# A mixing matrix from split factors: three products of rounded parts in place of one product in full precision

## The chip, the core and the metric

The kernel runs on one core of a Trainium2 chip. The metric is the device time of one execution in microseconds (us), taken as the median over several executions. A second number, the span, comes from one execution under the hardware profiler: it runs from the first to the last instruction of the program, and is a little shorter than the time of the same execution. Five engines work side by side, each through its own queue in order: the tensor engine (PE, with its weight loads shown apart as PEld), VectorE (DVE), ScalarE (ACT), GpSimd (POOL), and SyncE (SP), which here issues nearly all DMAs.

## The reference

The input x has four blocks (b) of 512 rows and 256 columns. Two layers follow each other, each of a mixer `s` and a gated feed-forward net `g`, joined as `x + s * silu(g)`.

```python
# layer 0, mixer: one step of a recurrence that starts from zero
xi = (x @ W_in.T).reshape(b, l, NC, D)[..., None]
nr, ni = B_real * xi, B_imag * xi          # the old state is zero
y = jnp.sum(C_real * nr - C_imag * ni, axis=-1)
out = y.reshape(b, l, NC * D) @ W_out.T
s = x + rmsnorm(out) * norm_w
# both layers, feed-forward net (fwht: a Walsh-Hadamard transform over the 1024 hidden columns)
hidden = fwht(silu(x @ W1.T) * (x @ W3.T))
g = hidden @ W2.T
```

Here x is already layer-normalized. Since the state begins at zero, the sum over the 16 state entries is a number for each of the 512 inner columns: `g[c] = sum(C_real * B_real - C_imag * B_imag)`. The mixer is therefore a single matrix of 256 by 256, `m = W_in.T @ diag(g) @ W_out.T`, which doesn't depend on x. The kernel computes m once, on the chip, and all four blocks use it. Layer 1 has an attention as its mixer.

## The kernel before, in words

**Split numbers.** Most products are made from pairs: a float32 array is rounded to a narrower matmul format (`F32R`), the high part, and the rest is stored as a low part of the same format. `split` (L59 to L62) does this with an ACT copy for the high part and a DVE subtraction for the low. `mm3` (L80) multiplies two pairs in three products: high by high, then high by low and low by high. In the profile all matmuls and transposes have the line L70 and all splits the lines L61 and L62, so that one goes by the names of tiles.

**Layer 0.** `ffn` treats one block in eight chunks of 128 hidden columns. For chunk c it makes two products (`f_0gu` and so on, the digit naming the block), puts a silu on one (L523), multiplies by the other (L524), splits the result into `hh` and `hl`, and feeds both to the down product `f_0dn`. Beside this, at two slots in each chunk, `Beside` runs steps of other tasks, in the given order, and spreads them by the counts that are passed with them.

In block 0 the first of these tasks is `prep_first`, which prepares weights. It is a generator made of two others:

- `prep_w2` applies the Hadamard transform to W2. For each half of its 256 columns it has three butterfly steps on DVE (`w2b`, L151 and L152), for the second half a split (`w2bh`, `w2bl`), and then two products by the Hadamard matrix (`w2ps`), each split into `w2h` and `w2l`.
- `prep_m` makes g on DVE (`cb` L203, `cbd` L205, `g` L207), scales the rows of W_out by it on ACT (`wg`, L210), and then calls `product_of_weights`: eight matmuls of plain float32 tiles (`mps<-wg,win`), and a split of the result into `mh` and `ml`.

After `prep_first` comes `mixer(0)`: it multiplies the block by m with `mm3` (`o`), copies the result to `osb` (ACT, L719), takes the squares of its rows on ACT (`junk`, L721), the power on POOL (`ssr`, L723 and L724), scales `osb` on DVE (L726) and adds it to `xn` (L729). Then `norm(0, 1)` normalizes block 1 (`ln_1st`, `xn`, L272 to L279), transposes it on PE (`xt_1tp`) and splits it into `xt`, the operand of all products of block 1. In block 0 four low halves of the hidden tiles (`early`, L540) are made late.

**Layer 1's weights.** While layer 0 runs, `prep_s` loads W1 and W3 of layer 1 in four quarters (`sraw`), adds and subtracts blocks (`ssum`), splits (`sp`) and writes the pairs to DRAM (`s<-sp`); `load_s` reads them back (`sw<-s`) into the buffers that the weights of layer 0 leave.

**What sets the order.** In layer 0 the program order is not the order of the queues. The kernel is built with a scheduler, which places the instructions on each engine by a model of times of its own; `after(...)` pins a few. A change in the program text can so rearrange queues far behind it. From the last down products of layer 0 on, PE's order is fixed by hand (`in_line`, L66 to L69). Buffers come from rings: tag `t4` has ten buffers of 4 KB for each partition (win, wout, wg, w2bh, sraw and many others), the PSUM tag `ms` three (`w2ps`, `mps`, `o`, the transposes), and `gu` three. A tile can be written only when the tile before it in its buffer has been read for the last time.

The order of the tasks around m, in `prep_first`, is:

```python
        for _ in range(2):
            next(steps)          # two of the butterfly steps of W2's second half
            yield
        product = prep_m(*raw_m)
        next(product)            # g and wg
        for _ in range(2):
            next(steps)          # third butterfly step; split into w2bh, w2bl
            yield
        load_x(1)
        next(product)            # mps, mh, ml
        yield
        yield from steps         # the two w2ps of the second half
```

Of the kernel before, what the change touches and what calls it, by code (L numbers as in the profile page):

```python
# [11 lines left out]
F32 = mybir.dt.float32  # L12
# [3 lines left out]
F32R = mybir.dt.float32r  # L16
AF = mybir.ActivationFunctionType
ALU = mybir.AluOpType
# [3 lines left out]
P = 128  # L22
D = 256
# [12 lines left out]
def kernel(ctx: ExitStack, tc: tile.TileContext, a: dict, out: bass.AP):  # L36
    nc = tc.nc

    wp = ctx.enter_context(tc.tile_pool(name="weights", bufs=1))
    act = ctx.enter_context(tc.tile_pool(name="act", bufs=2))  # L40
    dram = ctx.enter_context(tc.tile_pool(name="dram", bufs=2, space=bass.MemoryType.DRAM))
    ps = ctx.enter_context(tc.tile_pool(name="ps", bufs=2, space=PSUM))

    def t4(name, shape, dt=F32):
        return act.tile(shape, dt, tag="t4", name=name, bufs=10)
# [10 lines left out]
    def psum(name, shape, tag="ms", bufs=3):  # L56
        return ps.tile(shape, F32, tag=tag, name=name, bufs=bufs)

    def split(src, hi, lo, engine=nc.vector):  # L59

        h = nc.scalar.copy(hi, src)  # L61
        return h, engine.tensor_tensor(lo, src, hi.bitcast(F32), ALU.subtract)  # L62
# [5 lines left out]
    def in_line(call, *args, **kwargs):  # L68
        with tc.issue_after(line["last"].ins) if line["fixed"] and line["last"] else nullcontext():  # L69
            ins = call(*args, **kwargs)  # L70
        line["last"] = ins
        return ins

    def matmul(*args, **kwargs):
        return in_line(nc.tensor.matmul, *args, **kwargs)
# [4 lines left out]
    def mm3(o, terms):  # L80

        seq = [(l[0], r[0]) for l, r in terms]
        for l, r in terms:
            seq += [(l[0], r[1]), (l[1], r[0])]
        for n, (l, r) in enumerate(seq):
            ins = matmul(o, l, r, start=n == 0, stop=n == len(seq) - 1)
        return ins
# [4 lines left out]
    def x_slot(name, shape):  # L92
        return wp.tile(shape, F32, tag="x", name=name, bufs=B)

    def load_x(b, nt=NT, queues=(nc.sync,)):
        xs[b] = x_slot(f"x{b}", [P, NT, D])
        src = a["x"][b].rearrange("(t p) d -> p t d", p=P)
        for t in range(0, NT, nt):
            queue = queues[t // nt % len(queues)]
            queue.dma_start(xs[b][:, t : t + nt, :], src[:, t : t + nt, :])  # L100
# [38 lines left out]
    def prep_w2(layer, raws, dst, scratch):  # L139

        w2h, w2l = dst
        for half in range(2):
            ds_ = slice(half * P, (half + 1) * P)
            cur = raws[half]
            for st, h in enumerate((1, 2, 4)):
                nxt = scratch(f"w2b{st}_{layer}_{half}", [P, NH, P])
                cv = cur.rearrange("p (g two h) d -> p g two (h d)", two=2, h=h)
                nv = nxt.rearrange("p (g two h) d -> p g two (h d)", two=2, h=h)  # L150
                nc.vector.tensor_tensor(nv[:, :, 0], cv[:, :, 0], cv[:, :, 1], ALU.add)  # L151
                nc.vector.tensor_tensor(nv[:, :, 1], cv[:, :, 0], cv[:, :, 1], ALU.subtract)  # L152
                cur = nxt
                yield

            native = layer == 0 and half == 0
            if not native:
                bh = t4(f"w2bh_{layer}_{half}", [P, NH, P], F32R)
                bl = t4(f"w2bl_{layer}_{half}", [P, NH, P], F32R)
                split(cur, bh, bl)  # L160
                yield
            for q in range(2):
                o = psum(f"w2ps_{layer}_{half}_{q}", [P, NH // 2, P])
                qs = slice(q * NH // 2, (q + 1) * NH // 2)
                if native:
                    matmul(o, had_f, cur[:, qs, :], start=True, stop=True)
                else:
                    matmul(o, had, bh[:, qs, :], start=True, stop=False)
                    matmul(o, had, bl[:, qs, :], start=False, stop=True)
                split(o, w2h[:, qs, ds_], w2l[:, qs, ds_])  # L170
                yield
# [4 lines left out]
    def w2_tiles(layer):  # L176
        return w2_tile(f"w2h_{layer}"), w2_tile(f"w2l_{layer}")

    def product_of_weights(name, lhsT, rhs, nk):

        hi = wp.tile([P, 2, D], F32R, name=f"{name}h")
        lo = wp.tile([P, 2, D], F32R, name=f"{name}l")
        o = psum(f"{name}ps", [P, 2, D])
        for i in range(2):
            for k in range(nk):
                matmul(
                    o[:, i, :], lhsT(k, i), rhs(k), start=k == 0, stop=k == nk - 1
                )
        split(o, hi, lo)
        return hi, lo  # L190

    def load_m():
        win = t4("win", [P, 4, D])
        wout = t4("wout", [P, 4, D])
        nc.sync.dma_start(bc, a["bc"])
        nc.sync.dma_start(wout, a["w_outT"].rearrange("(c p) o -> p c o", p=P))
        nc.sync.dma_start(win, a["w_in"].rearrange("(c p) i -> p c i", p=P))
        return win, wout

    def prep_m(win, wout):  # L200

        cb = wp.tile([P, 4, 2, DS], F32, name="cb")
        nc.vector.tensor_tensor(cb, bc[:, :, 0:2, :], bc[:, :, 2:4, :], ALU.mult)  # L203
        cbd = wp.tile([P, 4, DS], F32, name="cbd")
        nc.vector.tensor_tensor(cbd, cb[:, :, 0, :], cb[:, :, 1, :], ALU.subtract)  # L205
        g = wp.tile([P, 4], F32, name="g")
        nc.vector.tensor_reduce(g, cbd, AX.X, ALU.add)  # L207
        wg = t4("wg", [P, 4, D])
        for c in range(4):
            nc.scalar.mul(wg[:, c, :], wout[:, c, :], g[:, c : c + 1])  # L210
        yield
        first["m"] = product_of_weights(
            "m", lambda k, i: win[:, k, i * P : (i + 1) * P], lambda k: wg[:, k, :], 4
        )
        yield

    def sl(i):
        return slice(i * P, (i + 1) * P)
# [240 lines left out]
    def after(ins):  # L459
        return tc.issue_after(ins.ins) if ins else nullcontext()  # L460
# [444 lines left out]
    def call(f, *args):  # L905
        f(*args)
        yield
# [26 lines left out]
    raw_m = load_m()  # L934
# [3 lines left out]
    first = {"table": None}  # L938
# [15 lines left out]
    def prep_first():  # L954
        steps = prep_w2(0, raw2, w2, x_slot)
        with after(first["w13"][1]):
            next(steps)
        yield
        for _ in range(4):
            next(steps)  # L960
            yield
        with after(first["silu"]):
            nc.scalar.copy(had, had_f)
        for _ in range(2):
            next(steps)
            yield
        product = prep_m(*raw_m)
        next(product)
        for _ in range(2):
            next(steps)  # L970
            yield
        load_x(1)
        next(product)
        yield
        yield from steps
# [15 lines left out]
    for b in range(B):  # L991
        tasks = []
        if b == 0:
            prep = prep_first()
            next(prep)
            tasks.append((prep, 11))
        if b:
            tasks.append((call(gate_all, f"g0_{b - 1}", dn, xns[0, b - 1], xs[b - 1]), 1))
        tasks.append((mixer(b), MIXER))
        if b + 1 < B:  # L1000
            if b:
                load_x(b + 1)
            if b == 2:
                tasks.append((prep_s(0), 4))
            tasks.append((norm(0, b + 1), NORM))
        if b == 0:
            early = w2_tile("early0"), w2_tile("early1")
            spare = [
                [early[i][:, 2 * c : 2 * c + 2, :].rearrange("p a d -> p (a d)") for i in range(2)]
                for c in range(NH // 2)  # L1010
            ]
        if b == 1:
            raw2_1 = load_w2(1)
            w2_1 = w2_tiles(1)
            tasks.append((prep_w2(1, raw2_1, w2_1, t4), W2P))
            tasks.append((prep_second(), 5))
        if b == 2:
            tasks += [(prep_s(1), 4), (norm(1, 0), NORM), (prep_s(2), 4)]
        if b == 3:
            atts = [Attention(0)]  # L1020
            at = atts[0]
            parts = run(at.xt_half, 0), run(at.xt_half, 1), at.xt, at.scaled, at.split_sums
            tasks += [(call(f), 1) for f in parts]
            norms = {1: norm(1, 1)}
            tasks.append((prep_s(3), 4))
        bg = Beside(*tasks)
        if b == 0:
            dn = ffn("f0_0", xTs[0, 0], w13, w2, bg.slot, NH, spare, parts=2, behind=True)
        else:
            tail = [run(atts[0].tq, j) for j in range(2)] if b + 1 == B else []  # L1030
            dn = ffn(f"f0_{b}", xTs[0, b], w13, w2, bg.slot, tail=tail)
        bg.finish()
# [33 lines left out]
    for b in range(B):  # L1066
# [15 lines left out]
        if not final:  # L1082
# [4 lines left out]
            c = Attention(b + 1)  # L1087
# [93 lines left out]
```

## Time and profile before

| what | value |
|---|---|
| time, median of 3 executions | 363.11 us (362.93 to 363.39) |
| the profiled execution: time | 362.72 us |
| the profiled execution: span | 360.9 us |
| DVE busy / ACT busy | 79% / 55% of the span |
| granted clock of PE | 1.00 throughout |
| eight products for m (`mps`), 16 records on PE | 26.4 to 31.4 us, beside other matmuls |
| `wg` on ACT, four of 128x256 | 24.65 to 26.36 us |
| split of m: `mh`, `ml` | 31.41 and 32.03 us |
| first product `o` with m | 36.34 us |
| first product of block 1 (`f_1gu`) | 51.49 us |
| loads of `sraw`, issued by SP | 82.41, 104.41, 132.84 and 158.48 us, landing 4.4 us later |

The page of a profile gives busy times by engine, and groups of instructions with their counts and mean lengths. The timeline lists instructions of one engine in order of time: start, length, engine, line, operation, the tile written and the tiles read, shape and count; in brackets the idle time of the engine before it and what ended it. The chain of waits follows the work that ended last back from the end: at each step to what released it, or to the instruction before it on its engine. An FP32 matmul shows as two records in this trace, a matmul of split numbers as one.

### The profile page before, as it was taken

Reading aid. Unit: us, or ns where it says so; the run is one execution under the profiler, and the core shown is the slowest. Engines: PE = TensorE matmul, PEld = TensorE weight load, DVE = VectorE, ACT = ScalarE, POOL = GpSimd, SP = SyncE. Lnnn points to the kernel's source line nnn. Section 1 sums busy time; section 2 is a strip of 40 time slices with the busy share of each in tenths; the row PEclk is TensorE's granted clock in tenths of the full one; section 3 lists DMA queues with packets and bytes.
Section 4 is the critical chain, followed back from the end, with each engine's and each line's share of the span. In section 5 each row is a group of like instructions: output and inputs, shape, how many; then the busy total and the mean of one; then the engine's idle time right before and its main releaser. Section 6 shows DMA issues by size and latency. Waiting matters only on the chain.

```text
span 360.9 us, 6262 instructions
## 1 busy us (share of the span) xinstructions
PE 354.3 (98%) x2469; PEld 327.9 (91%) x2469; DVE 286.1 (79%) x592; ACT 197.5 (55%) x372; POOL 19.0 (5%) x22
## 2 busy tenths in 40 slices
PE   8999999999999999999999999999999999999995
PEld 6878999888988898888999999999999999999995
DVE  6897868996679938898987957989679888568646
ACT  4665436274454335465467655576555676446443
POOL 1000201100011000100100001100011000000000
PEclk9999999999999999999999999999999999999999
DMA  7935000301063217637257135661554635345401
GB/s 228 346 108 186 3 0 2 116 0 60 0 196 155 118 52 236 237 130 254 85 206 261 49 157 205 223 226 79 203 205 152 215 162 203 136 149 193 194 2 58
DMA packets 16284, 52.25 MB, mean 145 GB/s; under 512 B 1632, under 2 KB 7936, under 8 KB 16256
## 3 DMA queue, kind: packets, MB, share of 16 engines
q1 hardware_dynamic: 15968, 51.60, 39.8%
q8 instruction: 19, 0.31, 0.3%
q10 hardware_dynamic: 288, 0.26, 0.2%
q14 instruction: 9, 0.07, 0.1%
HBM read 42.40 MB, written 9.45 MB: 144 GB/s over the span
## 4 chain that ended last, share of the span: by engine, by line
PE 78%; DVE 16%; ACT 2%; DMA 1%; issue 1%; POOL 1%; DVEq 0%; SPq 0%; ACTq 0%
PE f_0gu L70 6%; PE f_1gu L70 6%; PE f_0dn L70 5%; PE f_2dn L70 5%; PE f_3dn L70 5%; PE f_1dn L70 5%; PE f_3gu L70 5%; PE pv L70 4%; PE f_2gu L70 3%; PE tq L70 2%; PE o L70 2%; PE v L70 2%; PE sc L70 2%; PE warm L70 2%; DMA sraw<-in_w 1%; DVE sp L62 1%
## 5 line engine op out<-in xcount | busy, mean ns | idle before, releaser
L70 PE MATMUL f_3gu<-xt,w 128*128 128x512 f32 x96 | 25.6, 397 | 0.0
L70 PE MATMUL f_0gu<-xt,w 128*128 128x512 f32 (+1 forms) x108 | 24.9, 382 | 0.0
L70 PE MATMUL f_1gu<-xt,w 128*128 128x512 f32 x96 | 24.8, 395 | 0.0
L70 PE MATMUL f_2gu<-xt,w 128*128 128x512 f32 x96 | 24.6, 395 | 0.0
L70 PEld LDWEIGHTS f_0gu<-xt,w 128*128 128x128 f32 x108 | 18.6, 188 | 4.4 <-issue 1.0
L70 PEld LDWEIGHTS f_2gu<-xt,w 128*128 128x128 f32 x96 | 17.2, 188 | 3.2
L70 PEld LDWEIGHTS f_1gu<-xt,w 128*128 128x128 f32 x96 | 17.1, 188 | 3.2
L70 PEld LDWEIGHTS f_3gu<-xt,w 128*128 128x128 f32 x96 | 17.1, 188 | 2.9
L61 ACT CAST f_1hh<-f_1h 128x512 fp32r<-128x512 f32 x16 | 10.0, 623 | 16.7 <-DVE f_1h L524 13.6
L70 PE MATMUL f_1dn<-w2l,f_1hh 128*128 128x256 f32 x64 | 17.8, 282 | 0.0
L70 PE MATMUL f_2dn<-w2h,f_2hh 128*128 128x256 f32 x64 | 17.8, 283 | 0.0
L70 PE MATMUL f_1dn<-w2h,f_1hh 128*128 128x256 f32 x64 | 17.8, 281 | 0.0
L70 PE MATMUL f_2dn<-w2l,f_2hh 128*128 128x256 f32 x64 | 17.7, 283 | 0.0
L70 PE MATMUL f_3dn<-w2l,f_3hh 128*128 128x256 f32 x64 | 17.7, 282 | 0.0
L70 PE MATMUL f_3dn<-w2h,f_3hh 128*128 128x256 f32 x64 | 17.7, 281 | 0.0
L70 PE MATMUL f_3dn<-w2h,f_3hl 128*128 128x256 f32 x64 | 17.0, 283 | 0.4 <-DVE f_3hl L62 0.4
L70 PE MATMUL f_1dn<-w2h,f_1hl 128*128 128x256 f32 x64 | 17.1, 283 | 0.0
L70 PE MATMUL f_2dn<-w2h,f_2hl 128*128 128x256 f32 x64 | 16.8, 283 | 0.2 <-DVE f_2hl L62 0.2
L61 ACT CAST f_2hh<-f_2h 128x512 fp32r<-128x512 f32 x16 | 9.9, 621 | 12.4 <-DVE f_2h L524 9.1
L61 ACT CAST f_3hh<-f_3h 128x512 fp32r<-128x512 f32 (+1 forms) x17 | 10.1, 596 | 11.3 <-DVE f_3h L524 7.1
L62 DVE TENSOR_TENSOR f_2hl<-f_2h,f_2hh 128x512 fp32r<-128x512 f32 x16 | 10.9, 682 | 3.9 <-ACT f_2hh L61 3.8
L70 PE MATMUL f_0dn<-w2h,f_0hl 128*128 128x256 f32 x48 | 13.7, 284 | 0.1
(480 smaller groups left out, 1139.4 us busy)
## 6 DMA issues: line engine op xcount, KB each, us to landing
sw<-s SPq DMA_DIRECT2D x32, 896.0 KB, 5.5
s<-sp SPq DMA_DIRECT2D x8, 512.0 KB, 4.1
s<-sp SPq DMA_DIRECT2D x8, 384.0 KB, 2.5
w2raw<-in_w SPq DMA_DIRECT2D x4, 512.0 KB, 5.9
sraw<-in_w SPq DMA_DIRECT2D x4, 512.0 KB, 4.4
mrb<-there SPq DMA_DIRECT2D x4, 512.0 KB, 3.9
w13raw<-in_w SPq DMA_DIRECT2D x3, 512.0 KB, 6.6
x<-in_x SPq DMA_DIRECT2D x3, 512.0 KB, 3.4
```

What stands on the lines that cost most here:

```text
L61: h = nc.scalar.copy(hi, src)
L62: return h, engine.tensor_tensor(lo, src, hi.bitcast(F32), ALU.subtract)
L70: ins = call(*args, **kwargs)
```

## The change

`product_of_weights` goes. `prep_m` now makes pairs of both factors: `wgh` is the old ACT product written in the narrow format, `wgl` is `wout * g - wgh` on DVE, and `win` is split into `wih` and `wil`. The product is made by `mm3` for each half i of the rows, over four k: 24 matmuls of split numbers in place of eight in float32. The first step of `prep_m` is moved from behind the second butterfly step to behind the split of W2's second half and `load_x(1)`. Between it and the product of m now stands the first `w2ps` of the second half. The count passed for the task goes from 11 to 12. The pairs take four buffers of the ring `t4` where `wg` took one.

```diff
-        wg = t4("wg", [P, 4, D])
+        wg = [t4(f"wg{i}", [P, 4, D], F32R) for i in "hl"]
+        wi = [t4(f"wi{i}", [P, 4, D], F32R) for i in "hl"]
         for c in range(4):
-            nc.scalar.mul(wg[:, c, :], wout[:, c, :], g[:, c : c + 1])
-        yield
-        first["m"] = product_of_weights(
-            "m", lambda k, i: win[:, k, i * P : (i + 1) * P], lambda k: wg[:, k, :], 4
-        )
+            nc.scalar.mul(wg[0][:, c, :], wout[:, c, :], g[:, c : c + 1])
+            nc.vector.scalar_tensor_tensor(
+                wg[1][:, c, :], wout[:, c, :], g[:, c : c + 1], wg[0][:, c, :].bitcast(F32),
+                ALU.mult, ALU.subtract,
+            )
+        split(win, *wi)
+        yield
+        hi, lo = (wp.tile([P, 2, D], F32R, name=f"m{i}") for i in "hl")
+        o = psum("mps", [P, 2, D])
+        for i in range(2):
+            mm3(
+                o[:, i, :],
+                [(tuple(z[:, k, sl(i)] for z in wi), tuple(z[:, k, :] for z in wg)) for k in range(4)],
+            )
+        split(o, hi, lo)
+        first["m"] = hi, lo
         yield
...
-        product = prep_m(*raw_m)
-        next(product)
         for _ in range(2):
             next(steps)
             yield
         load_x(1)
+        product = prep_m(*raw_m)
+        next(product)
+        yield
+        next(steps)
+        yield
         next(product)
         yield
         yield from steps
...
-            tasks.append((prep, 11))
+            tasks.append((prep, 12))
```

More of the change, by code (lines that the diff above doesn't have):

```diff
@@ L177, in w2_tiles @@
         return w2_tile(f"w2h_{layer}"), w2_tile(f"w2l_{layer}")
[L179 to L187, printed above, removed]
-                )
-        split(o, hi, lo)
-        return hi, lo
     def load_m():
@@ L207, in prep_m @@
         nc.vector.tensor_reduce(g, cbd, AX.X, ALU.add)
-        wg = t4("wg", [P, 4, D])
+        wg = [t4(f"wg{i}", [P, 4, D], F32R) for i in "hl"]
+        wi = [t4(f"wi{i}", [P, 4, D], F32R) for i in "hl"]
         for c in range(4):
-            nc.scalar.mul(wg[:, c, :], wout[:, c, :], g[:, c : c + 1])
-        yield
-        first["m"] = product_of_weights(
-            "m", lambda k, i: win[:, k, i * P : (i + 1) * P], lambda k: wg[:, k, :], 4
-        )
+            nc.scalar.mul(wg[0][:, c, :], wout[:, c, :], g[:, c : c + 1])
[4 more added lines that the diff above has]
+        split(win, *wi)
+        yield
+        hi, lo = (wp.tile([P, 2, D], F32R, name=f"m{i}") for i in "hl")
[7 more added lines that the diff above has]
+        first["m"] = hi, lo
         yield
```

## The prediction, made before the changed kernel was run

> **What bounds the kernel now.** I read the busy row of the page first, then the slices of the span, then the tensor engine (PE) in order of time, then the chain of waits where that row shows a hole.
>
> ```profile
> PE 354.3 (98%) x2469; PEld 327.9 (91%) x2469; DVE 286.1 (79%) x592; ACT 197.5 (55%) x372; POOL 19.0 (5%) x22
> ```
>
> PE is busy in 98% of the span, but a matmul's recorded end overlaps the next one's start, so the row alone doesn't say that PE is saturated. I therefore took the distance from each matmul's start to the next: a 128x512 split product follows the last after 0.233 us, a 128x256 one after 0.119, almost everywhere. The product that the change concerns stands in this timeline of PE:
>
> ```profile
> 26.37 0.59 PE L70 MATMUL mps<-wg,win 128*128 128x256 f32 x2
> 26.61 1.05 PE L70 MATMUL f_0gu<-xt,w 128*128 128x512 f32 x3
> 27.50 1.03 PE L70 MATMUL mps<-wg,win 128*128 128x256 f32 x4
> 28.18 1.04 PE L70 MATMUL f_0gu<-xt,w 128*128 128x512 f32 x3
> 29.06 2.32 PE L70 MATMUL mps<-wg,win 128*128 128x256 f32 x10
> 31.03 0.81 PE L70 MATMUL w2ps<-w2bh,had 128*128 128x512 f32 x2
> 31.68 1.56 PE L70 MATMUL f_0gu<-xt,w 128*128 128x512 f32 x6
> ```
>
> There is no hole in it: PE goes from one group straight into the next. So what is taken off PE here is worth its full length, unless a wait appears. From 31.68 to 113 us the spacing shows no hole over 0.1 us either. The first real ones in layer 0 are these, from the chain of waits (start, length, engine and tile):
>
> ```profile
> 112.59 0.84 DVE sp L62
> 113.43 0.16 DVE ln_3mv L274 x2
> 113.59 0.58 DVE f_2hl L62
> 114.17 0.04 issue
> 114.22 1.22 PE f_2dn L70 x8
> ...
> 158.48 5.35 DMA sraw<-in_w
> ...
> 169.88 0.60 DVE tql L62
> 170.48 0.15 DVE ln_1mv L274 x2
> 170.64 0.59 DVE f_3hl L62
> 171.23 0.04 issue
> 171.27 1.46 PE f_3dn L70 x10
> ```
>
> In both PE waits for the low half of a hidden tile, made late by VectorE (DVE). At 114.22 the spacing before f_2dn is 0.38 too long, and 0.11 more follows: 0.49. At 171.27 it is 0.58 and 0.11: 0.69. The second goes back to the load of sraw, which DVE awaited for 1.5 us.
>
> **What the Trainium skill says.** "FP8 and Floating Point Precision", TensorE Precision Notes: true FP32 takes four passes through the array. The split form takes three products. The trace agrees nearly: 0.43 us for an FP32 128x256 product (below) against 0.119 for a split one, a factor of 3.6. "Perfetto Trace Analysis", Identifying the Most-Contended Engine: matmul busy time is no good measure of saturation. The trace agrees; hence the start-to-start spacing.
>
> **The change part by part.**
>
> *PE.* Between 26.37 and 31.68 lie 5.31 us, with 6 f_0gu (6 x 0.233 = 1.40) and two w2ps of the same width (0.46). The rest, 3.45 us, is the eight FP32 products, which the trace shows as 16 records. The new form has 2 x 4 x 3 = 24 split products of 128x256. The same shape is in the trace:
>
> ```profile
> 88.37 1.43 PE wqkps L70 x12
> ```
>
> So 24 take 2.86, and PE saves 0.59 us. As that row measures this very operation, its error is some 0.05.
>
> *DVE and ScalarE (ACT).* DVE gets four wgl (nearest row: the four osb of 128x256 at L726, 1.67 us together) and one wil of 1024 columns (like w2bl, 1.2): 2.9 us. ACT gets wih (like w2bh, 1.05); its four wg stay. They stand in full queues, so I walked each engine's queue in the changed program's own instruction order, with durations and spacings of the trace (DVE 0.60 from one 128x512 to the next). Up to 26.37 the PE queue is the old one. DVE then has w2bl until 27.7, f_0hl and f_0h of chunks 4 and 5 until 28.9, wgl until 30.5, wil until 31.7. ACT has wgh from 26.65, when g is ready, to 28.35, wih to 29.4, then w2h and f_0hh, and the silu of chunk 6 until 31.65. PE reaches the first product of m at 31.03 (needs wih: 1.6 us spare), the first with wgl at 31.5 (1.0 spare), the last f_0gu at 32.3 (needs that silu: 0.7 spare), and those with wil at 33.7 (2.0 spare). So the cover holds, and the new DVE and ACT work costs nothing here. DVE had 4.4 us of idle time between 26.4 and 44 (17.6 less 13.2 busy). Without that cover its 2.9 us would show on PE.
>
> *What moves: the mixer of block 0.* m is now complete at about 36.0 instead of 31.4, and the o products, at 36.3 before, now stand in the PE queue behind most of the down products: their last starts at 45.5. This is the part with a price. The old walk through it, from DVE and ACT's timelines:
>
> ```profile
> 41.72 0.17 DVE L723 TENSOR_SCALAR ssr<-ssr 128x4 f32<-128x4 f32 x1 [0.18 <-ACT junk L721]
> 42.66 1.38 DVE L279 TENSOR_SCALAR xn<-x,ln_1mv,ln_1r 128x256 f32<-128x256 f32 x4 [0.77 <-POOL ln_1r L277]
> 43.96 1.67 DVE L726 SCALAR_TENSOR_TENSOR osb<-osb,ssr,nwb 128x256 f32<-128x256 f32 x4
> 45.66 1.23 DVE L729 TENSOR_TENSOR xn<-xn,osb 128x1024 f32<-128x1024 f32 x1
> 47.71 1.29 DVE L62 TENSOR_TENSOR xt<-xt_1tp,xt 128x512 fp32r<-128x512 f32 x2 [0.82 <-ACT xt L61]
> ```
>
> The low halves of xt were ready at 49.0, and block 1 began at 51.49: 2.5 us to spare. Now: o ends at 45.75; ACT copies it until 46.4 and squares three tiles (0.54 each) until 48.05; ssr 48.2; POOL's power about 1.1, to 49.35; osb to 51.05; the add to 52.25; the low halves of xt at 52.9 and 53.5. The transposes are also later: the two PSUM buffers that they need are freed only by ml and by the copy of o, and they now stand among the last twelve down products. Their last pair starts at 50.4; ACT starts on xt 0.31 later (47.09 after 46.78 before) and has the first high half at 51.3. PE, 0.59 ahead, would begin block 1 at 50.9: it waits 0.48. After 1.74 us of products on high halves it wants the first low half, at 53.1, against 52.9: just in time. Cost: 0.48, between 0.2 (the transposes run a little earlier) and 1.3 (POOL and DVE each some tenths late). Behind that wait on PE stands all of block 1; behind xt on DVE the gate g_0g and f_1h, which PE wants 2 us after they come.
>
> *The two later stalls.* The scheduler has rearranged the queues downstream. At 113 DVE did two ssum (0.67) and a sp (0.84) between the add and f_2hl. In the changed order they stand behind f_2hl. It then ends at about 112.4, wanted at 113.7: 0.49 saved. At 171 the load of the last sraw stood on SP's queue behind a weight load that had to await a free buffer until 158.38. Now it stands directly behind the one issued at 149.19, so it lands near 154 (its 4.4 us). DVE no longer idles, and f_3hl can end near 170.0, by f_3h at 166.2, four statistics (1.3), tql after the interleaved tq at 169.2, one pair of aggregates and itself. PE wants it at 170.6: 0.69 saved. Either may turn up as another wait: 0 to 1.18 together; I take all.
>
> *Other queues.* Three more tiles of the ten-buffer ring go round. The second w2raw load of layer 1 now awaits wil (31.7 rather than issue at about 30), but is used after 55. The load of x(1) waits for the same w2b operation as before, and POOL's order is unchanged. Layer 1's PE order is fixed by hand and the same but for one neighbouring swap. These cost nothing.
>
> Sum: -0.59 + 0.48 - 0.49 - 0.69 = -1.29. The profiled execution spans 360.9 and took 362.72, so 1.8 lie outside the span; it would become 361.4. The median of the runs shown is 363.11, or 0.39 above it: 361.8.
>
> **Rivals.**
> *Only the arithmetic* (chance 0.20): the stalls at 114 and 171 move but don't go, as a rearranged queue makes others. For it: DVE is full at both, 85% between 100 and 113.6 and all of 164 to 171.3. Against: the walk above has 1.3 and 0.6 spare. 363.11 - 0.59 + 0.48 = 363.0.
> *The mixer's tail becomes the bound* (0.16): on DVE the low halves of xt stand behind ssr, osb and the add. Every us that this tail runs later than walked is a us of PE at the start of block 1, and DVE carries its lag into the f_1h of that block. For it: the tail crosses PE, ACT, DVE and POOL, five handovers that I price at 0.05 to 0.2 each, and had 2.5 us to spare before against 0.2 now. Against: in the old trace each step took what I use. From a tail 1.3 us late with the later stalls unchanged: 363.0 + 1.3 = 364.3. It decides from 0.15 us late where the stalls stay, from 1.3 where they go.
> *The new form saves nothing* (0.02): 24 products as dear as 8. The wqkps row excludes it but for interleaving losses; with the later stalls 363.11 + 0.48 = 363.6.
>
> **How the numbers follow.** The forecast has 0.62. What a measurement can tell from no change is 0.2%, 0.73 us: faster is below 362.4, slower above 363.8. The forecast's own range is 361.3 to 362.5, nearly all of it faster. Some of the rivals' weight spills over: the arithmetic alone is mostly "same". Faster 0.64, same 0.20, slower 0.16. The 8-in-10 range takes in the arithmetic alone and the lower ends of the unknowns: 361.1 to 363.4.
>
> **What would show it.** Right: mps x24 spaced at 0.119; f_1gu starting near 51.4, released by ACT's xt; no hole at f_2dn near 114 or f_3dn near 171; the last sraw issued near 149. Wrong: a PE wait on DVE's xt over 0.5 us in block 1, a hole before the f_0gu of chunk 7 near 32, or new waits for f_1hl, f_2hl or f_3hl.

## The result and the profile after

| | before | after |
|---|---|---|
| median of the timed executions | 363.11 us | 361.18 us (360.98 to 361.50) |
| ratio to before, 95% interval | | 0.9947 [0.9936, 0.9958] |
| profiled execution: time / span | 362.72 / 360.9 us | 361.18 / 359.4 us |
| PE busy | 98%, 2469 matmul records | 98%, 2477 |
| DVE busy | 79% of the span | 80% |

The kernel became 1.9 us faster; 361.8 was predicted. The spans differ by 1.5.

A part of each span varies from one execution to the next: the first f_0gu starts at 7.67 us in the profile before, and at 7.83 and 8.02 in two profiles of the changed kernel (the second is after_again, below). From there to the start of the last matmul it is 348.73 us before and 347.04 after (348.87 and 347.02 in the second profiles), so 1.7 to 1.9 less.

The readings below follow the prediction's terms; a "wait" is always the excess of the distance from one matmul's start to the next over the usual distance of that shape.

*The product.* From the timeline of PE after the change (start, length, engine, line, operation, tiles, shape, count):

```profile
29.74 1.56 PE L70 MATMUL f_0gu<-xt,w 128*128 128x512 f32 x6
31.14 0.64 PE L70 MATMUL mps<-wgh,wih 128*128 128x256 f32 x4
31.61 0.28 PE L70 MATMUL mps<-wgl,wih 128*128 128x256 f32 x1
31.73 0.39 PE L70 MATMUL w2ps<-w2bh,had 128*128 128x512 f32 x1
31.96 0.40 PE L70 MATMUL w2ps<-w2bl,had 128*128 128x512 f32 x1
...
32.43 1.56 PE L70 MATMUL f_0gu<-xt,w 128*128 128x512 f32 x6
33.83 0.28 PE L70 MATMUL mps<-wgh,wil 128*128 128x256 f32 x1
...
35.99 0.28 PE L70 MATMUL mps<-wgh,wil 128*128 128x256 f32 x1
```

The products from 31.14 to 31.61 stand 0.118 us apart, and nothing waits in this stretch: the operands made by DVE and ACT were there in time. The 24 products take 2.86 us.

*The start of block 1.* The timelines of PE, ACT and DVE after the change (in brackets: idle time before the instruction, and what ended it):

```profile
50.55 0.38 PE L70 MATMUL xt_1tp<-ident,xn 128*128 128x128 f32 x2
...
50.88 0.28 PE L70 MATMUL f_0dn<-w2h,f_0hl 128*128 128x256 f32 x1
51.49 0.74 PE L70 MATMUL f_1gu<-xt,w 128*128 128x512 f32 x2 [0.33 <-ACT xt L61]
```

```profile
50.85 1.07 ACT L61 CAST xt<-xt_1tp 128x512 fp32r<-128x512 f32 x2 [0.66 <-PE xt_1tp L70]
```

```profile
48.04 0.17 DVE L722 TENSOR_SCALAR ssr<-ssr 128x4 f32<-128x4 f32 x1 [5.17 <-ACT junk L720]
49.33 1.67 DVE L725 SCALAR_TENSOR_TENSOR osb<-osb,ssr,nwb 128x256 f32<-128x256 f32 x4 [1.12 <-POOL ssr L723]
51.04 1.22 DVE L728 TENSOR_TENSOR xn<-xn,osb 128x1024 f32<-128x1024 f32 x1
52.18 1.28 DVE L62 TENSOR_TENSOR xt<-xt_1tp,xt 128x512 fp32r<-128x512 f32 x2
```

From 50.88 to 51.49 is 0.61, where a 128x256 product takes 0.12: PE waits 0.49 for ACT's first high half, and 0.11 more follows at the first f_1gu. The first low half is ready on DVE at 52.9, and no wait for the low halves follows.

*The two later waits.* The DVE timeline near 112 us, the load queue (SP) near 149, and PE's part of the chain of waits (start, length, engine, tile):

```profile
112.06 0.24 DVE L273 BATCH_NORM_AGGREGATE ln_3mv<-ln_3st 128x2 f32<-128x6 f32 x2
112.22 0.66 DVE L62 TENSOR_TENSOR f_2hl<-f_2h,f_2hh 128x512 fp32r<-128x512 f32 x1
112.80 0.42 DVE L329 TENSOR_TENSOR ssum<-sraw 128x256 f32<-128x256 f32 x1
```

```profile
148.68 0.32 SPq L349 DMA_DIRECT2D sw<-s  x1
149.05 0.42 SPq L324 DMA_DIRECT2D sraw<-in_w  x1
156.58 0.32 SPq L349 DMA_DIRECT2D sw<-s  x1
```

```profile
112.62 1.39 PE f_2gu L70 x6
114.01 0.95 PE f_2dn L70 x8
...
166.81 1.86 PE tq L70 x8
168.66 2.83 PE f_3dn L70 x24
```

f_2hl now stands ahead of the sums and ends at 112.9, over a microsecond before f_2dn uses it; before, the chain went through `sp` and f_2hl here. Before, the load queue read (the two weight loads in one line started at 149.19 and 158.06):

```profile
149.19 9.19 SPq L350 DMA_DIRECT2D sw<-s  x2
158.48 0.38 SPq L325 DMA_DIRECT2D sraw<-in_w  x1
```

The last sraw is now issued at 149.05 instead of 158.48, and the chain near 170, which went through that load and a row of DVE instructions, is PE alone.

*One more.* Adding up the excess spacing of PE in stretches of 10 us, one further difference over 0.2 us appears: before, the tq products waited 0.28 at 301; after, they don't.

### The profile page after: what moved, and what is told of

Read it like the earlier page. It is cut to its first block, busy times and chain, and to the rows that moved or that the text cites. A ratio compares the mean times of both kernels' runs of the same rounds, so it can differ in the third digit from the quotient of the medians.

```text
span 359.4 us, 6279 instructions
## 1 busy us (share of the span) xinstructions
PE 352.8 (98%) x2477; PEld 327.2 (91%) x2477; DVE 287.5 (80%) x597; ACT 197.9 (55%) x373; POOL 20.8 (6%) x22
## 4 chain that ended last, share of the span: by engine, by line
PE 85%; DVE 12%; ACT 1%; DMA 1%; POOL 1%; issue 0%; DVEq 0%
PE f_0gu L70 6%; PE f_1gu L70 6%; PE f_2gu L70 6%; PE f_3gu L70 6%; PE f_3dn L70 6%; PE f_2dn L70 6%; PE f_0dn L70 5%; PE f_1dn L70 5%; PE pv L70 4%; PE o L70 3%; PE tq L70 3%; PE v L70 2%; PE sc L70 2%; PE w2ps L70 1%; PE pt L70 1%; DVE neg L814 1%
```

## The experiments

Two theories at the start. Mine: the terms of the prediction are separate (arithmetic, the wait at block 1, the two later waits), each with its own cause. The rivals: the gain comes from the new form alone; or DVE is so full that a wait taken away at one place returns at the next. Each kernel was timed 5 to 21 times beside the kernel before, which took 362.88 us in the set of e1 to e5, 362.94 in that of e6, e7 and after_again, and 363.10 in that of e8 to e10. Each ratio is to the kernel before of its own set.

| run | edit | median, us | ratio to before | span |
|---|---|---|---|---|
| e1_position | FP32 product, new place and count | 362.58 | 0.9992 [0.9984, 1.0000] | 360.8 |
| e2_form | split product, old place and count | 362.64 | 0.9992 [0.9984, 1.0001] | 361.1 |
| e4_sraw | before, load order | 361.85 | 0.9975 [0.9964, 0.9986] | 360.0 |
| e5_sums | before, load and DVE order | 361.39 | 0.9959 [0.9946, 0.9971] | 359.4 |
| e6_norm_first | after, xt of block 1 ahead of the mixer | 362.65 | 0.9992 [0.9984, 1.0000] | 361.1 |
| e7_all | e6 with the pins of e5 | 361.04 | 0.9949 [0.9937, 0.9962] | 359.3 |
| after_again | the changed kernel | 361.30 | 0.9956 [0.9943, 0.9968] | 359.6 |
| before_again | the kernel before, one profile | 362.86 (one) | | 361.1 |
| e8_low_half | e7 with one add moved | 360.77 | 0.9936 [0.9923, 0.9948] | 358.9 |
| e9_fp32_queues | e7 with the FP32 product | 361.28 | 0.9950 [0.9936, 0.9964] | 359.9 |
| e10_double | e7 with the product made twice | 363.56 | 1.0013 [1.0006, 1.0019] | 361.6 |

### The two halves of the change alone

e1_position moves the FP32 product:

```diff
-        product = prep_m(*raw_m)
-        next(product)
         for _ in range(2):
             next(steps)
             yield
         load_x(1)
+        product = prep_m(*raw_m)
+        next(product)
+        yield
+        next(steps)
+        yield
...
-            tasks.append((prep, 11))
+            tasks.append((prep, 12))
```

> The kernel before with its FP32 product, but at the new place in the preparation (two steps later) and with the new count of 12 steps; only the position changes. My theory (three separate terms): the eight FP32 products still take 3.45 us; o and the transposes of xt come late as in the changed kernel, so block 1 waits 0.5 to 0.6 us for ACT's xt near 52; the last load of sraw and the sums of the second quarter keep their places, so the waits near 114 (0.5) and 171 (0.7) stay. Time 363.1 + 0.6 = 363.7. Rival (the placement is what gains): the waits at 114 or 171 go, 362.5 or less. Rival (any rearrangement moves the time by chance): waits of some tenths at places not named here.

e2_form has the new `prep_m` at the old place with the old count, that is, the first part of the change's diff without the rest.

> The kernel before with the split factors and the three passes, but at the old place and with the old count of 11; only the form changes. My theory: 24 products in 2.86 us instead of 3.45, so PE gains 0.59; but here the cover is thin: ACT has wih between wgh and w2bh, so w2bh ends near 28.9 where PE wants it near 28.3, a new wait of about 0.5 (0.2 to 0.9) before the w2ps; no wait at the start of block 1, and both later waits (0.5 near 114, 0.7 near 171) stay. Time 363.1 - 0.6 + 0.5 = 363.0 (362.7 to 363.4). Rival (the gain of the change is arithmetic alone): no wait at the w2ps and 361.2 to 362.5. Rival (chance): the later waits differ from those of before although the queues there are the same.

Each half alone moved the time by 0.3 us or less, the whole by 1.6 to 1.9: the halves don't add. In both, the waits near 114 and 171 are as before (e1: 0.51 and 0.75; e2: 0.49 and 0.86), and so are SP's order and DVE's near 112. Of these kernels only the one with both edits has the later queues rearranged.

For e1 my expectation was wrong at block 1. The views of PE around the last transposes of xt and the start of block 1, in e1:

```profile
47.06 0.38 PE L70 MATMUL xt_1tp<-ident,xn 128*128 128x128 f32 x2
...
51.54 0.28 PE L70 MATMUL f_0dn<-w2h,f_0hl 128*128 128x256 f32 x1
51.66 1.09 PE L70 MATMUL f_1gu<-xt,w 128*128 128x512 f32 x4
```

The last transposes are 3.5 us earlier than after the change, and block 1 starts without a wait. In e1 the o products stand from 36.8 to 42.2, after the change from 39.2 to 45.7. There the low part of m was ready at 39.6, but the first product that reads it is at 43.35: the scheduler had put down products between. So the new place alone doesn't make the wait. In e1 the low part is ready at 35.9, so m's time and the order both differ from the changed kernel; e6 and e7 keep m's high part late and change the order.

For e2 the expected wait is there. PE and ACT in e2:

```profile
27.96 0.64 PE L70 MATMUL mps<-wgh,wih 128*128 128x256 f32 x4
28.44 0.28 PE L70 MATMUL mps<-wgl,wih 128*128 128x256 f32 x1
29.14 0.74 PE L70 MATMUL w2ps<-w2bh,had 128*128 128x512 f32 x2 [0.42 <-ACT w2bh L61]
```

```profile
26.58 1.03 ACT L61 CAST wih<-win 128x1024 fp32r<-128x1024 f32 x1
27.52 0.61 ACT L61 CAST f_0hh<-f_0h 128x512 fp32r<-128x512 f32 x1
28.04 1.04 ACT L61 CAST w2bh<-w2b 128x1024 fp32r<-128x1024 f32 x1
```

wih stands ahead of w2bh on ACT, and PE waits 0.58 and 0.11 for w2bh: 0.69, against 0.59 saved. At the old place the form has no cover and gives everything back. The time, 362.64, is just under the expected 362.7 to 363.4; the kernel before was 0.2 lower in this set too. The move behind W2's split is what hides the new operand work.

### The two later waits, without the product

e4_sraw pins the weight load behind the last load of sraw:

```diff
-        nc.sync.dma_start(raw, a["w13_1"][q])
+        sloads[q] = nc.sync.dma_start(raw, a["w13_1"][q])
...
-            nc.sync.dma_start(parts[i].bitcast(F32), sdram[q][i])
+            with after(sloads[3] if n == 1 else None):
+                nc.sync.dma_start(parts[i].bitcast(F32), sdram[q][i])
```

> The kernel before with one order on the load queue changed: the last load of sraw ahead of the weight load that waits for a free buffer. My theory: sraw is issued near 149 instead of 158.5, VectorE no longer idles for it, and the wait of PE for f_3hl near 171 (0.69) goes: 363.1 - 0.7 = 362.4; the wait near 114 stays. Rival (the load is hidden anyway, VectorE is full there): the wait stays or turns up elsewhere within 10 us, 363.1. If the weight load, now later by one issue, is the one that is missed: a new wait of PE near 180, 363.1 or more.

e5_sums pins the sums and the first split of the second quarter behind the low half of f_2 (`hls` collects the low halves as they are made):

```diff
+        with after(hls[-3] if q == 1 else None):
             nc.vector.tensor_tensor(s1, a21, a22, ALU.add)
             nc.vector.tensor_tensor(s3, a11, a21, ALU.subtract)
...
-            split(src[:, :n, :], *parts)
+            nc.scalar.copy(parts[0], src[:, :n, :])
+            with after(hls[-4] if q == 1 and at == 0 else None):
+                nc.vector.tensor_tensor(parts[1], src[:, :n, :], parts[0].bitcast(F32), ALU.subtract)
```

> The kernel before with the sums and the split of the second quarter of sraw pinned behind the f_2hl that PE waits for near 114; the load of the last sraw comes ahead of the weight load in this order as well, so it has both edits on the later queues. My theory: both waits go (0.49 and 0.69): 363.1 - 1.2 = 361.9, and against e4_sraw 0.5 less. Rival (VectorE is full, the work pushed back makes the next low half late): only one of them gains, 362.4 to 362.6. Rival (chance): no gain, 363.1.

Both came out by my theory. Against the kernel before of their set they gained 1.03 and 1.49 us, 0.3 more than the 0.69 and 1.18 of its sums, which left out the wait at 301 (it is absent here too). In e4 the load queue and the chain read:

```profile
149.25 0.32 SPq L351 DMA_DIRECT2D sw<-s  x1
149.67 0.38 SPq L325 DMA_DIRECT2D sraw<-in_w  x1
158.13 0.32 SPq L351 DMA_DIRECT2D sw<-s  x1
```

```profile
112.66 0.84 DVE sp L62
114.28 1.22 PE f_2dn L70 x8
...
168.35 0.93 PE tq L70 x4
169.28 0.94 PE f_3dn L70 x8
170.69 1.42 PE f_3dn L70 x12
```

The wait near 171 is gone and the one near 114 stays. In e5 the second is gone too, as after the change:

```profile
112.63 1.39 PE f_2gu L70 x6
114.02 0.94 PE f_2dn L70 x8
...
168.67 2.83 PE f_3dn L70 x24
```

e5 takes 1.5 us off the kernel before with the FP32 product untouched at its old place. The rival of a full DVE, where what is pushed back makes the next low half late, falls for these two waits. These two waits are most of what the change gained.

### The wait at block 1

e6_norm_first lets the transposes for block 1 go ahead of the mixer in the changed kernel:

```diff
-        tasks.append((mixer(b), MIXER))
+        if b:
+            tasks.append((mixer(b), MIXER))
...
             tasks.append((norm(0, b + 1), NORM))
+        if not b:
+            tasks.append((mixer(b), MIXER))
```

> The changed kernel with one swap: in block 0 the normalisation and the transposes for block 1 go ahead of the mixer, so xt of block 1 no longer waits behind the o products and their tail. In this order the load of the last sraw is back behind the weight load, and the sums of the second quarter are back ahead of f_2hl. My theory: the wait of 0.6 at the start of block 1 goes, but the waits near 114 (0.5) and 171 (0.7) are back. From the changed kernel 361.2 - 0.6 + 1.2 = 361.8, so slower than it although the wait that my prediction was about is gone. The first f_1h now stands behind osb and the add on VectorE; if that is late for PE, up to 1 us more at 54 to 58. Rival (what the change gained is the arithmetic): 360.6.

e7_all is e6_norm_first with the pins of e5_sums.

> The kernel of e6_norm_first with the pins of e5_sums: split product, xt of block 1 ahead of the mixer, the second quarter's sums behind f_2hl, the last sraw ahead of the weight load. My theory: no wait near 51, 114 or 171, only the arithmetic's gain and the two later ones: from before -0.59 - 0.49 - 0.69, with the wait near 301 gone too -0.28, in all 2.05: 360.8 to 361.0, and 0.4 to 0.6 under the changed kernel. If the first f_1h is late, up to 1 us is lost again near 55. Rival (VectorE is full, so what is saved at one place is lost at the next): 361.2 to 361.8.

after_again and before_again are the two given kernels.

> The changed kernel once more, on the chip of the two runs above, for comparison with them: 0.9947 of before, about 361.0 if before is 362.9; its wait of 0.6 near 51 shows again, none near 114, 171 and 301.

> The kernel before once more, for a second profile: the waits near 114 (0.49) and 171 (0.69) show again. The wait near 301 (0.28) is in its first profile and in none of the four edited kernels; if it belongs to the kernel it shows again, if it was an accident of that one execution it doesn't.

after_again shows the 0.60 near 51 and none of the others. before_again has 0.49 near 114, 0.81 near 171 and 0.30 near 301: the one near 171, 0.69 in the first profile, varies by 0.1 from one execution to the next.

In e6 the product is where it is after the change. The high part of m is ready at 37.2 (36.9 after the change) and the low part at 38.3 (39.6). PE's last transposes and the start of block 1 in e6:

```profile
43.77 0.39 PE L70 MATMUL xt_1tp<-ident,xn 128*128 128x128 f32 x2
...
51.47 2.96 PE L70 MATMUL f_1gu<-xt,w 128*128 128x512 f32 x12
```

The transposes stand 6.8 us earlier than after the change, and the wait at block 1 is gone: with m's high part as late, the order decides. The later two waits are back, as its queues said, and the time is before's less 0.3, where I had expected 361.8. The wait near 114 was larger than I had priced, 0.75, and the one that I had expected at 54 to 58 came at 71, where PE waits 0.33 for an f_1hl. e7 has that one too, and one of 0.21 near 39, for a low half made late (`early`); it has none near 51, 114, 171 or 301. I had expected it 0.4 to 0.6 us under the changed kernel. It is 0.26 under after_again, less than the two intervals can tell apart, and the traces show no gain: 347.08 us from the first f_0gu to the start of the last matmul, against 347.04 and 347.02. So for this swap the rival of a full DVE came true in e7: of the 0.60 that it took away, 0.54 came back as waits for low halves near 39 and 71. DVE in e7 near 70:

```profile
68.95 0.68 DVE L152 TENSOR_TENSOR w2b<-w2raw 128x512 f32<-128x512 f32 x1
69.55 1.22 DVE L731 TENSOR_TENSOR xn<-xn,osb 128x1024 f32<-128x1024 f32 x1
70.68 0.16 DVE L275 TENSOR_SCALAR ln_2r<-ln_2mv 128x4 f32<-128x4 f32 x1
70.75 0.68 DVE L62 TENSOR_TENSOR f_1hl<-f_1h,f_1hh 128x512 fp32r<-128x512 f32 x1
```

An add of 1.22 us, which nobody needs soon, stands ahead of the low half that PE could use at 71.26. e8_low_half moves the mixer's last add of block 1 behind it:

```diff
+        if b == 1:
+            yield            # four times
...
-        nc.vector.tensor_tensor(xn, xn, osb, ALU.add)
+        with after(hls[-1] if b == 1 else None):
+            nc.vector.tensor_tensor(xn, xn, osb, ALU.add)
...
-            tasks.append((mixer(b), MIXER))
+            tasks.append((mixer(b), MIXER + 4 * (b == 1)))
```

> The kernel of e7_all, with the mixer's last add of block 1 put behind the f_1hl that PE waited for near 71 (0.33). My theory: VectorE reaches that f_1hl 1.2 earlier (the add's length), so the wait goes and nothing else moves: e7_all less 0.3, 360.7, about 2.2 under before. Rival (VectorE is full, the wait only moves on): the add turns up as a wait of PE within the next 30 us, 361.0.

```profile
69.41 0.66 DVE L62 TENSOR_TENSOR f_1hl<-f_1h,f_1hh 128x512 fp32r<-128x512 f32 x1
69.98 1.22 DVE L737 TENSOR_TENSOR xn<-xn,osb 128x1024 f32<-128x1024 f32 x1
```

The low half ends 1.4 us earlier, the wait near 71 is gone, and no later one takes its place; of the one near 39, 0.10 is left. So near 71 it was the order on DVE, and not its fullness, that made the wait. e8 is the fastest kernel of the study: 2.3 us under before.

### The arithmetic by itself

e9_fp32_queues puts the old `product_of_weights` into e7_all; e10_double loops over `(0, 0, 1, 1)` where the product loops over `range(2)`.

> The kernel of e7_all with the FP32 product of the kernel before in place of the split one: all the edits of the queues, without the form. My theory: the form is worth its arithmetic, 3.45 - 2.86 = 0.59, on PE; 361.04 + 0.59 = 361.6 if the wait near 71 is there too, 361.3 if it isn't (VectorE has 2.9 us less to do). Rival (the form saves nothing, as the FP32 products leave room for other engines to catch up): 361.0.

> The kernel of e7_all with the 24 split products made twice (each half of m is computed two times over into the same place). My theory: PE is the bound at this place, so its work counts in full: 24 x 0.119 = 2.86 more, 363.9, perhaps 0.3 less as the wait near 71 may find VectorE further on. Rival (PE has room here, other engines set the pace): under 1.5 more.

Neither has the wait near 71, so both compare with e8. e9 is 0.51 us slower than e8 (361.23 to 361.75 against 360.72 to 360.86). e8 alone has the 0.10 near 39, so the arithmetic's 0.59 should show as 0.49. Their queues differ in other places too, but in no other does the excess spacing differ by over 0.1. e10 is slower than e8 by 0.0077 of 363, or 2.8 us: its 48 products take 5.74 us in the spacing, 2.88 more than the 24 of e8, and 2.88 less the same 0.10 is 2.78. Work on PE counts in full here; the rivals that PE has room, or that the new form saves nothing, fall.

## Why the prediction was right, and what it missed

| term | predicted | in the traces | shown by |
|---|---|---|---|
| eight FP32 products become 24 split ones | -0.59 | 2.86 us in the spacing; 0.5 in time | e9 against e8, e10 |
| no wait on operands in block 0 | 0 | 0 | trace of after; e2 shows the wait without the move |
| block 1 waits for xt | +0.48 | +0.60 | trace of after; absent in e1, e6, e7, e8 |
| f_2hl ahead of the sums | -0.49 | wait gone | e5 |
| last sraw ahead of the weight load | -0.69 | wait gone | e4, e5 |
| tq at 301 | not in the sum | -0.28 | both profiles of before, none of the others |

*Right.* The arithmetic, the cover, and both later waits came as worked out, and f_1gu began at 51.49 where 51.4 was said. (The walk to 171 gave the last sraw 4.4 us to land. That is the landing of the first sraw; in the chain of before the last one takes 5.35. It made no difference: f_3hl ended at 169.4 after the change, where 170.0 was said.) The first and third terms cancel: what the change does directly is worth about nothing. The gain comes from two queues 80 to 140 us further on, which shifted because the scheduler had other work to place. The prediction had read this from the changed order, so it was no luck there; for the change itself it was: e6 holds the whole change, and a swap of two tasks brings both waits back. "Only the arithmetic", 363.0, falls with e5; "the mixer's tail becomes the bound" didn't happen: the low halves of xt on DVE, which it named, came in time, and PE waited for ACT's first high half, behind the last transposes.

*Missed.* 361.8 was 0.6 above 361.18, and three terms make this up. The step "1.8 lie outside the span ... the median of the runs shown is 363.11, or 0.39 above it" carried 0.39 over to the changed kernel, whose median equalled its profiled time; the profiled execution of before was 0.2 under the fastest of those that its median was taken from, and its first f_0gu came 0.16 earlier than in the profile after. The wait near 301 wasn't in the sum, 0.28. And the wait at block 1 was mis-sized by 0.12: I had it between ACT's first high half and PE, and the first f_1gu lost 0.11 more. For both later waits I had counted such a second part, but not for this one. 361.8 - 0.39 - 0.28 + 0.12 is 361.25.

*The reason given for the wait at block 1.* I called it the price of m being complete later. The path that I walked, from late transposes over ACT's first high half to PE, is the one in the trace, and its number was near because I had read it from the changed order itself. That m's lateness is the root isn't shown. In e6 and e7 the high part is as late and there is no such wait; after the change the low part was ready 3.7 us before the first product that reads it. On the other hand before, e1 and e2, which also have the mixer first, have m complete at 32.7, 35.9 and 33.7 and no wait, so m's time may be why the scheduler placed the o products and the transposes late.

*Open.* The wait near 301 goes back to a DVE instruction near 295, `f_2v`: from it on DVE has no idle time up to the `xgl` that the tq product reads (301.75 in the first profile, where that product starts at 301.80). In the second profile of before, PE and DVE read:

```profile
293.73 0.86 PE L70 MATMUL f_2gu2z<-tb,sw 128*128 128x256 f32 x6
```

```profile
294.09 0.68 DVE L768 TENSOR_TENSOR xf<-xf,mrb 128x512 f32<-128x512 f32 x1
295.07 0.69 DVE L648 TENSOR_TENSOR f_2v<-f_2gu2z,f_2v 128x512 f32<-128x512 f32 x1 [0.30 <-ACT tb L61]
```

f_2v starts 1.34 us after the first of the f_2gu2z that it reads, and 1.32 in the first profile; in all other profiles it is 0.97. The semaphores that it awaits are the same in all. It is in both profiles of before and in no other kernel, and it is of the size of e1's gain, for which I have no other reason. What causes it isn't settled.

## What to carry to other kernels

Where a scheduler sets the queues, price an edit from the new order of every engine, far behind the edit too: here the direct effect was about zero, and two waits 80 to 140 us later decided. Such waits can be had by pins without the edit, and a gain of this kind says nothing for the edit itself: try the halves alone before crediting either. After each wait removed, look for the next low half that PE awaits and for what long, unhurried instruction stands ahead of it on DVE.

## What the hardware showed that I had not expected

An FP32 128x256 matmul is two records 0.2155 us apart. Where a split product follows, the last of the records stands only 0.03 before it, and that next product seems 0.19 too long (26.59, 26.61 and 27.03 in the kernel before). The sum is unchanged, so this is how the records are placed and not a cost of switching. e9 against e8 agrees, with 0.51 us measured where the spacing gives 0.49.

A wait of PE costs a little more than the wait. In all thirteen profiles, every wait of 0.14 to 0.70 us from 40 us on is followed by a second spacing that is 0.10 to 0.11 too long, whatever the length of the wait: at 114.22 it is 0.38 and then 0.10, at 171.27 0.58 and 0.11, at 191.12 (in block 0 of layer 1) 0.26 and 0.10. With these second parts, the waits that e5 is free of add up to 1.46 us, without them to about 1.15; e5 gained 1.49 in time (1.0 to 2.0 by its interval) and 1.54 to 1.68 from the first f_0gu to the last matmul. So the second parts look like lost time, as far as one kernel can show it.
